# Two single-batch groups at the ends of a 16-batch pipeline, and the last batch's keys and values behind the batch ahead of it

## The chip, the core and the metric

The kernel runs on one core of a Trainium2 chip. The metric is device time in microseconds (us), the median of the runs of the whole program; lower is better. Before the change it is 1442.21 us (three runs, 1441.21 to 1450.63). Engine names are those of the profile: PE is TensorE (matmuls), PEld its weight loads, DVE is VectorE, ACT is ScalarE, POOL is GpSimd, SP is SyncE, which issues nearly all transfers.

## The reference, cut to what matters

Two layers work on 16 batches of 112 tokens with 512 channels, all in float32. Layer 0 is cross-attention from the tokens to 375 context rows of the same batch; layer 1 is one recurrent block (RWKV-like) over the 112 tokens.

```python
# layer 0: 16 heads of 32
a = layer_norm(ctx) * gamma + beta
Q, K, V = x @ Wq.T, a @ Wk.T, a @ Wv.T
x = x + tanh(gate) * (softmax(Q K^T * scale, masked) V) @ Wo.T
# layer 1: 32 heads of 16, state s of 16 x 16 for each head
xa = ln(x, ln1);  sx = shift(xa) - xa            # "front"
xxx = tanh((xa + sx * maa_x) @ maa_w1) @ maa_w2   # five mixes
xk, xw, xv, xr, xg = xa + sx * (maa_stack + xxx)
w = exp(-exp(time_decay + tanh(xw @ td_w1) @ td_w2))
r, k, v, g = xr @ Wr.T, xk @ Wk.T, xv @ Wv.T, silu(xg @ Wg.T)
out_t = r_t . (u * k_t v_t + s);  s = k_t v_t + w_t * s   # "middle", over 112 tokens
x1 = x + (group_norm(out) * g) @ Wo.T             # "back"
xc = ln(x1, ln2);  xk2, xr2 = mixes of xc and its shift
return x1 + sigmoid(xr2 @ Wfr.T) * (relu(xk2 @ Wfk.T)**2 @ Wfv.T)
```

A batch depends on no other batch. Nothing in a layer-1 stage can start before layer 0 has finished for all batches of its group.

## The kernel before, in words

**Tiles.** Tokens lie along the free dimension and channels along the 128 partitions, in four chunks (`NC`). Layer 1 works on groups of `GB` = 2 batches, so on `N` = 224 columns; there are `NG` = 8 groups. A 512 x 512 weight is used in two halves; each call of `project` (L175) loads one half (512 KB, a "slab", five buffers) and runs 8 products, each of which the profile shows as two PE instructions, 16 in all. Ten weights go through `project`: `wq`, `wo` (layer 0), `wk1`, `wv1`, `wr1`, `wg1`, `wo1`, `wfk`, `wfr`, `wfv` (layer 1). A group thus takes 20 calls and 320 instructions.

**Attention** (`attention`, L383) goes batch by batch in four steps of four heads. The context of the batch ahead is turned, and its keys and values are made, in eleven units (`context_units`, L214: four turns, four keys, three values) that are dealt out over the four steps of the current batch; queries of the next group join them (`query_units`, L261). Scores run at L301, transposes of the probabilities at L332, outputs at L351, keys at L237, values at L248. When the last batch of a group has been divided by its sums (`divide`, L358), `project_units` (L274) applies `wo` for the group and adds to `x` at L281; from then on layer 1 of the group may begin.

**Layer 1** has three stages, each a generator for a group: `front` (L517: norm, shift, five mixes), `middle` (L648: four projections, then 16 steps `n`), and `back` (L835: second half of the group norm, `wo1`, second norm, `wfk`, `wfr`, `wfv`, output). A step of `middle` reads a value row back from DRAM spread over 16 partitions (four transfers on SP, L722), multiplies it by the keys (L735, half on DVE and half on POOL), runs the recurrence as scans (L758 on DVE, two scans of two columns with 2 x 224 elements each), multiplies by `r` (L762 on POOL) and sums by matmul (L774). The wide tiles of `front` and `back` have one buffer for each name, so a group's second norm (tile "kk", L848) waits until the group ahead has used its own "kk" in `wfv`.

**Order.** One loop (L919) writes out all work in one sequence. Every generator yields costs; each of the four strands (attention, front, middle, back) has a place on one axis, and the strand with the smallest place goes next. Attention moves 1/92 for each unit of cost (`ATT`), a stage moves its length divided by its listed cost: lengths 0.35, 0.75, 0.8 for front, middle, back (L41). A stage of group g starts no earlier than the place where the stage before it ended, and each strand does one group at a time. For the group ahead of the last, `AHEAD_OF_LAST` (L43) shortens front to 0.25 and middle to 0.6. The framework lays out each engine's static order from this sequence; an instruction whose inputs are ready can be put ahead of earlier ones that are not. `planned_after` adds order without a wait. SP issues weights, contexts and the spreads of L722 in one queue.

Of the kernel before, what the change touches and what calls it, by code (L numbers as in the profile page):

```python
# [18 lines left out]
GB = 2  # L19
NG = B // GB  # L20
# [22 lines left out]
AHEAD_OF_LAST = {"front": 0.25, "middle": 0.6}  # L43
# [6 lines left out]
def xattn_rwkv_kernel(ctx: ExitStack, tc: tile.TileContext, ins: dict, out: bass.AP):  # L50
    nc = tc.nc

    def planned_after(later, earlier):

        tc.add_manual_dep(
            later.ins, earlier.ins.name,
            mybir.DependencyInfo(
                mybir.DependencyClass.NoSync, mybir.DependencyReason.SCHED_ONLY
            ),
            reason="room in the static order",  # L60
        )

# [73 lines left out]
    def load_x(g):  # L136
        xt = xp.tile([P, NC, N], F32, tag="x", name=f"x_{g}")
        nc.sync.dma_start(xt, ins["x"][:, :, g * N : (g + 1) * N])
        return xt

    def load_first():

        xt = xp.tile([P, NC, N], F32, tag="x", name="x_0")
        w = slabs.tile([P, NC, 2 * P], F32, tag="slab", name="wq_0")
        for k in range(NC):
            nc.sync.dma_start(xt[:, k, :], ins["x"][:, k, 0:N])
# [28 lines left out]
    def project(name, mm, rhs, label):  # L175

        w = first.pop(0) if first else slab(name, mm)
        ps = mm_tile(label)
        for e in range(2):
            for k in range(NC):  # L180
                mm_ = nc.tensor.matmul(  # L181
                    ps[:, e * N : (e + 1) * N], w[:, k, e * P : (e + 1) * P], rhs[:, k, :],
# [4 lines left out]
        return ps[:, : 2 * N].rearrange("p (e n) -> p e n", e=2)  # L187
# [73 lines left out]
    def query_units(g):  # L261
        qTs[g] = qT = kvp.tile([P, NC, N], F32, tag="qT", name=f"qT_{g}")
# [26 lines left out]
    def scores(b, m):  # L289
# [6 lines left out]
        qT, kT, mb, t0 = qTs[b // GB], kTs[b][m], masks[b], (b % GB) * T  # L296
# [61 lines left out]
    def divide(b, oR):  # L358
# [16 lines left out]
        t0 = (b % GB) * T  # L375

        with tc.high_priority(AHEAD):
            nc.vector.tensor_tensor(
                qTs[b // GB][:, :, t0 : t0 + T], pb[:, : NC * T].rearrange("p (m t) -> p m t", m=NC), oR,
# [3 lines left out]
    def attention():  # L383
# [3 lines left out]
        for cost, unit in queries[:1] + keys_values[:2] + queries[1:] + keys_values[2:]:  # L387
# [5 lines left out]
        for i in range(NC * B + 2):  # L393
            b, m = divmod(i, NC)
            if i < NC * B:
                if m == 0:
                    g = b // GB
                    if b % GB == 0 and g + 1 < NG:
                        xg[g + 1] = load_x(g + 1)
                    if b + 1 < B:  # L400
                        units += context_units(b + 1)
                        if (b + 1) % GB == 0:
# [6 lines left out]
                yield 0.9  # L409
            copied = None  # L410
# [5 lines left out]
            if i < NC * B:  # L416
# [3 lines left out]
            todo = -(-len(units) // (NC - m)) if i < NC * B else len(units)  # L420
            mine, units = units[:todo], units[todo:]
            mine = mine + [(0.0, lambda: None)] * (3 - len(mine))
            if ready and bm == NC - 1:
# [5 lines left out]
                if bb % GB == GB - 1:  # L429
                    mine = mine[1:2] + project_units(bb // GB) + mine[2:]  # L430
# [15 lines left out]
            before = (b, m, prs) if i < NC * B else None  # L446
# [5 lines left out]
    def wide(tag, name, bufs=1):  # L452
        return big.tile([P, NC, N], F32, tag=tag, name=name, bufs=bufs)

    def duo(tag, name, bufs=2):
        return chk.tile([P, 2, N], F32, tag=tag, name=name, bufs=bufs)

    def small(name):
        return tmp.tile([P, 2, N], F32, tag="tmp", name=name)
# [18 lines left out]
    def over_chunks(t):  # L478
        return t.unsqueeze(1).broadcast_to([P, NC, N])

    def layer_norm(src, dst, sq, late, name):
# [11 lines left out]

        halves(dst, src)
        yield 2.5
        mean = mm_tile(f"{name}_mean")[:, :N]
# [7 lines left out]
        var = mm_tile(f"{name}_var")[:, :N]  # L504
        total(var, sq)
        yield 1
        r = inverse_std(flat(small(f"{name}_r"))[:, :N], var)
        for cc in range(2):
            d2 = dst[:, two(cc), :]
            nc.vector.tensor_tensor(d2, d2, r.unsqueeze(1).broadcast_to([P, 2, N]), ALU.mult)  # L510
# [6 lines left out]
    def front(g):  # L517

        x = xg[g]
        xa, sx = wide("xa", f"xa_{g}"), wide("sx", f"sx_{g}")  # L520
        yield from layer_norm(x, xa, wide("mx", f"sq_{g}"), g == NG - 1, f"ln1_{g}")
        for c in range(NC):
# [9 lines left out]
            by_batch(sx)[:, :, :, 0], st01[:, 1, :, g * GB : (g + 1) * GB],  # L532
# [3 lines left out]
        mix = wide("mx", f"mx_{g}")  # L536
# [7 lines left out]
        for k in range(NC):  # L544
            nc.tensor.matmul(
                ps[:, :N], maa1[:, k, 0 : 4 * DM], mix[:, k, :], start=(k == 0), stop=(k == NC - 1)
# [477 lines left out]
```

## Time and profile before

| what | value |
|---|---|
| median of the runs | 1442.21 us |
| profiled execution, its own time | 1444.43 us |
| its span, first to last instruction | 1442.7 us |
| PE busy | 1344.5 us, 93% |
| DVE busy | 916.1 us, 63% |
| ACT, POOL busy | 658.8 and 660.8 us, 46% each |
| mean granted PE clock | 0.968 |
| moved by DMA | 171.80 MB, mean 119 GB/s |

Stages, read from when the lines ran: the first front follows the first `project_units` of layer 0 (L281 at 135 us); scans of the eight groups begin at 203, 355, 523, 688, 856, 1024, 1186 and 1316 us. In the steady part a group takes 167 us. The last group's L281 is at 1235 us, its scans run 1316 to 1394, and the program ends at 1442.7. Busy time of PE is the sum of modelled durations; the idle rest of the span is 98.2 us.

### The profile page before, as it was taken

Reading aid. Unit: us, or ns where it says so; the run is one execution under the profiler, and the core shown is the slowest. Engines: PE = TensorE matmul, PEld = TensorE weight load, DVE = VectorE, ACT = ScalarE, POOL = GpSimd, SP = SyncE. Lnnn points to the kernel's source line nnn. Section 1 sums busy time; section 2 is a strip of 40 time slices with the busy share of each in tenths; the row PEclk is TensorE's granted clock in tenths of the full one; section 3 lists DMA queues with packets and bytes.
Section 4 is the critical chain, followed back from the end, with each engine's and each line's share of the span. In section 5 each row is a group of like instructions: output and inputs, shape, how many; then the busy total and the mean of one; then the engine's idle time right before and its main releaser. Section 6 shows DMA issues by size and latency. Waiting matters only on the chain.

```text
span 1442.7 us, 23371 instructions
## 1 busy us (share of the span) xinstructions
PE 1344.5 (93%) x8516; PEld 953.6 (66%) x8516; DVE 916.1 (63%) x1750; ACT 658.8 (46%) x1527; POOL 660.8 (46%) x643
## 2 busy tenths in 40 slices
PE   7999998999999999999999999999999898789767
PEld 5557575757686677757676575866777476568546
DVE  1344647883768656774667837785658647884852
ACT  1444532564435653464435634365434446412342
POOL 3001335642546346552556335553456426664750
PEclk9999999999999999999999999999999999889979
DMA  7112035413545045522655035440544033435541
GB/s 233 57 52 82 2 103 153 152 47 97 163 146 162 30 143 170 154 87 73 181 155 158 31 109 173 131 155 30 175 156 156 32 104 126 157 110 150 174 139 57
DMA packets 114666, 171.80 MB, mean 119 GB/s; under 512 B 9768, under 2 KB 87464, under 8 KB 114296
## 3 DMA queue, kind: packets, MB, share of 16 engines
q1 hardware_dynamic: 113912, 169.69, 38.3%
q8 instruction: 67, 1.10, 0.3%
q10 hardware_dynamic: 576, 0.52, 0.1%
q14 instruction: 47, 0.39, 0.1%
q0 software_dynamic: 64, 0.10, 0.0%
HBM read 162.95 MB, written 7.34 MB: 118 GB/s over the span
## 4 chain that ended last, share of the span: by engine, by line
PE 68%; DVE 13%; DMA 5%; ACT 5%; POOL 4%; issue 3%; SPq 2%; DVEq 0%; POOLq 0%; ACTq 0%
PE pk L237 9%; PE pv L248 9%; PE pt L332 5%; PE ps L301 5%; DVE st L758 4%; PE pfv L181 3%; PE pfr L181 3%; PE po L181 3%; PE acc L774 3%; PE pq L181 3%; DMA kv<-vd 3%; PE pfk L181 3%; PE pr L181 2%; PE po L351 2%; PE pv L181 2%
## 5 line engine op out<-in xcount | busy, mean ns | idle before, releaser
L762 POOL TENSOR_TENSOR st<-st,r 128x448 f32<-128x448 f32 x256 | 321.4, 1270 | 213.1 <-DVE st L758 202.8
L758 DVE TENSOR_TENSOR_SCAN st<-wp,kv 128x448 f32<-128x448 f32 x256 | 268.1, 1077 | 112.1 <-ACT qT L268 33.3
L735 POOL TENSOR_TENSOR kv<-kv,k 128x444 f32<-128x444 f32 x128 | 153.4, 1201 | 92.0 <-DMA kv<-vd 90.0
L237 PE MATMUL pk<-aT,wk 128*128 128x375 f32 x512 | 181.6, 499 | 11.7 <-ACT oR L356 10.8
L248 PE MATMUL pv<-wv,aT 128*125 128x512 f32 x384 | 175.0, 599 | 1.4 <-ACT v L253 0.9
L312 DVE CUSTOM_DVE_ANT_0 pr<-ps,mb 112x375 f32<-112x375 f32 x256 | 128.1, 543 | 56.4 <-PE ps L301 56.2
L321 ACT ACTIVATE pr<-pr,mn 112x375 f32<-112x375 f32 x256 | 153.3, 602 | 4.8 <-DVE mn L312 4.6
L237 PEld LDWEIGHTS pk<-aT,wk 128*128 128x128 f32 x512 | 96.5, 196 | 69.6 <-ACT oR L356 12.6
L332 PEld LDWEIGHTS pt<-ident,pr 112*125 112x125 f32 x768 | 104.1, 192 | 36.8 <-issue 16.3
L332 PE MATMUL pt<-ident,pr 112*125 112x112 f32 x768 | 115.1, 281 | 6.1 <-DVE xm L562 5.7
L248 PEld LDWEIGHTS pv<-wv,aT 128*125 128x125 f32 x384 | 68.4, 187 | 77.2 <-issue 73.9
L735 DVE TENSOR_TENSOR kv<-kv,k 128x444 f32<-128x444 f32 x128 | 108.4, 847 | 1.4 <-DMA kv<-vd 1.3
L774 PE MATMUL acc<-st,consts 128*32 128x224 f32 x1024 | 78.0, 373 | 10.9 <-POOL st L762 9.4
L301 PE MATMUL ps<-kT,qT 32*112 32x375 f32 x512 | 84.1, 521 | 1.8 <-DVE xm L562 0.9
L470 ACT ACT_TABLE_LOAD x64 | 82.1, 1283 | 1.1
L568 POOL TENSOR_TENSOR xm<-xm,xa 128x448 f32<-128x448 f32 x48 | 59.0, 1244 | 37.6 <-DVE xm L562 37.5
L341 DVE COPY prT<-pt 125x448 f32<-125x448 f32 x80 | 49.2, 615 | 42.0 <-PE pt L332 41.9
L339 ACT COPY prT<-pt 125x448 f32<-125x448 f32 x112 | 59.1, 528 | 28.2 <-PE pt L332 28.1
L293 POOL TENSOR_SCALAR mb<-mrow 112x375 f32<-112x375 uint8 x16 | 8.9, 558 | 131.4 <-DVE mn L312 128.0
L562 DVE SCALAR_TENSOR_TENSOR xm<-pxm,vecs,sx 128x224 f32<-128x224 f32 x128 | 47.4, 443 | 28.2 <-PE pxm L585 28.1
L243 ACT COPY kT<-pk 128x375 f32<-128x375 f32 x64 | 30.1, 470 | 73.1 <-PE pk L237 72.4
L181 PE MATMUL pfk<-xk,wfk 128*128 128x224 f32 x256 | 53.8, 362 | 9.8 <-DVE xk L861 4.2
(146 smaller groups left out, 2367.2 us busy)
## 6 DMA issues: line engine op xcount, KB each, us to landing
kv<-vd SPq DMA_DIRECT2D x512, 111.5 KB
wo<-in_wo SPq DMA_DIRECT2D x32, 512.0 KB
ctx<-in_ctx SPq DMA_DIRECT2D x15, 750.0 KB
wv<-in_wv SPq DMA_DIRECT2D x16, 512.0 KB
wk<-in_wk SPq DMA_DIRECT2D x16, 512.0 KB
wr<-in_wr SPq DMA_DIRECT2D x16, 512.0 KB
wg<-in_wg SPq DMA_DIRECT2D x16, 512.0 KB
wfk<-in_wfk SPq DMA_DIRECT2D x16, 512.0 KB
```

The lines of the kernel that those rows point to most:

```text
L181: mm_ = nc.tensor.matmul(ps[:, e * N : (e + 1) * N], w[:, k, e * P : (e + 1) * P], rhs[:, k, :], start=(k == 0), stop=(k == NC - 1),)
L237: nc.tensor.matmul(pk[:, :S], wk[:, k, m * P : (m + 1) * P], aT[:, k, :], start=(k == 0), stop=(k == NC - 1),)
L248: nc.tensor.matmul(pv[:SC, :], aT[:, k, c * SC : (c + 1) * SC], wv[:, k, :], start=(k == 0), stop=(k == NC - 1),)
L301: score = nc.tensor.matmul(ps[:T, :S], qT[r : r + HD, m, t0 : t0 + T], kT[r : r + HD, :], start=True, stop=True,)
L312: nc.vector.tensor_tensor_reduce(pr, pss[hh][:T, :S], mb, 1.0, 3.0e38, ALU.add, ALU.min, mn)
L321: exp = nc.scalar.activation(pr, pr, AF.Exp, bias=mns[b][:, h : h + 1], scale=-1.0, accum_out=dens[b][:, h : h + 1],)
L332: nc.tensor.transpose(pt[:SC, hh * T : (hh + 1) * T], prs[hh][:, c * SC : (c + 1) * SC], ident[:T, :T])
L470: nc.scalar.preload_act_table_set(table)
L735: product = engine.tensor_tensor(kv4[:, two(p), :, 1:T], kv4[:, two(p), :, 1:T], k_prev.unsqueeze(1).broadcast_to([P, 2, GB, T - 1]), ALU. ...
L758: scan = nc.vector.tensor_tensor_scan(flat(pair), w_ps[c], flat(kv[:, two(p), :]), 0.0, ALU.mult, ALU.add)
L762: nc.gpsimd.tensor_tensor(pair, pair, rs[c // 2][:, c % 2, :].unsqueeze(1).broadcast_to([P, 2, N]), ALU.mult,)
L774: part = nc.tensor.matmul(accs[c][32 * q : 32 * q + 32, :], consts[:, C_WIN + 32 * e : C_WIN + 32 * e + 32], st[:, q, :], start=(e == 0), ...
```

## The change

Groups now have sizes 1, 2, 2, 2, 2, 2, 2, 2, 1: nine groups, {0}, {1,2}, {3,4}, ..., {13,14}, {15}. Everything that had 224 columns has 112 in the first and last group. A scan still works on 448 elements: for one batch it takes four columns at once (`nw` = 4), so a step of `middle` has one scan and one product with `r` instead of two. The number of spread transfers (four a step) and of slabs (20 a group) stays, so there are 64 more spreads, of half the size, and 20 more slabs than before.

The last batch's context units and its group's queries are no longer dealt out over the steps of batch 14. They are written after batch 14's last step: three in the first of two step-less turns of the loop, ten in the second: one ahead of `divide`, one between it and the two `project_units` calls of group {13,14}, eight behind these. Batch 14's steps carry no such units.

In the planner, the shortened lengths hold for two groups, {11,12} and {13,14}, and are 0.2 and 0.5; lengths of a one-batch group are halved. At the start, both query calls are written ahead of the first turns.

```diff
-GB = 2
-NG = B // GB
+SIZES = (1, 2, 2, 2, 2, 2, 2, 2, 1)
+NG = len(SIZES)
+FIRST = [sum(SIZES[:g]) for g in range(NG)]
+GROUP = [g for g in range(NG) for _ in range(SIZES[g])]
+GB = max(SIZES)
...
-AHEAD_OF_LAST = {"front": 0.25, "middle": 0.6}
+AHEAD_OF_LAST = {"front": 0.2, "middle": 0.5}
+AHEAD_OF = (NG-3, NG-2)
+
+SINGLE = 0.5
...
+        nt = rhs.shape[-1]
         for e in range(2):
             for k in range(NC):
                 mm_ = nc.tensor.matmul(
-                    ps[:, e * N : (e + 1) * N], w[:, k, e * P : (e + 1) * P], rhs[:, k, :],
+                    ps[:, e * nt : (e + 1) * nt], w[:, k, e * P : (e + 1) * P], rhs[:, k, :],
...
-        for cost, unit in queries[:1] + keys_values[:2] + queries[1:] + keys_values[2:]:
+        for cost, unit in queries + keys_values:
...
-        for i in range(NC * B + 2):
-            b, m = divmod(i, NC)
-            if i < NC * B:
-                if m == 0:
-                    g = b // GB
-                    if b % GB == 0 and g + 1 < NG:
+
+        steps = [divmod(i, NC) for i in range(NC * (B - 1))] + [None, None]
+        steps += [(B - 1, m) for m in range(NC)] + [None, None]
+        for i, step in enumerate(steps):
+            b, m = step or (B - 1, NC - 1)
+            if step:
+                if m == 0 and b < B - 1:
+                    g = GROUP[b]
+                    if b == FIRST[g] and g + 1 < NG:
                         xg[g + 1] = load_x(g + 1)
-                    if b + 1 < B:
+                    if b + 1 < B - 1:
                         units += context_units(b + 1)
-                        if (b + 1) % GB == 0:
+                        if b + 1 == FIRST[g] + SIZES[g]:
                             units += query_units(g + 1)
...
+            elif i < len(steps) - 2 and not units:
+                units = context_units(B - 1) + query_units(NG - 1)
...
+            if step is None and steps[i + 1 : i + 2] == [None]:
+                todo = min(3, todo)
...
+        gb, nt = SIZES[g], SIZES[g] * T
+        nw = NQ // gb
...
-            for p in range(2):
-                pair = st[:, two(p), :]
+            for p in range(NQ // nw):
+                columns = slice(p * nw, (p + 1) * nw)
+                pair = st[:, columns, :]
                 scan = nc.vector.tensor_tensor_scan(
-                    flat(pair), w_ps[c], flat(kv[:, two(p), :]), 0.0, ALU.mult, ALU.add
+                    flat(pair), w_ps[c], flat(kv[:, columns, :]), 0.0, ALU.mult, ALU.add
                 )
...
+    def length_of(name, g, length):
+        if g in AHEAD_OF:
+            length = AHEAD_OF_LAST.get(name, length)
+        return length * (1.0 if SIZES[g] == GB else SINGLE)
```

## The prediction

> **What bounds the kernel now.** I began with the page: the busy table, then the slices.
>
> ```profile
> PE 1344.5 (93%) x8516; PEld 953.6 (66%) x8516; DVE 916.1 (63%) x1750; ACT 658.8 (46%) x1527; POOL 660.8 (46%) x643
> ...
> PE   7999998999999999999999999999999898789767
> ...
> PEclk9999999999999999999999999999999999889979
> ```
>
> PE is the bound, and from the second slice to about the 32nd it has no room: work added there is paid in full, stalls of other engines hardly matter. Idle PE lies at the two ends. To size it I asked for busy time by stage, cut at the points where the stages change hands (columns: length, busy time and instructions of PE, PEld, DVE, ACT, POOL, granted clock, DMA share, GB/s).
>
> ```profile
> 0.00:40.00 40.00, 31.63 (x91) 20.07 (x92) 7.67 (x21) 7.79 (x15) 12.37 (x36) 0.91 0.76 234
> 40.00:1110.00 1070.00, 1037.19 (x6768) 725.97 (x6767) 694.02 (x1394) 520.26 (x1244) 480.31 (x461) 0.99 0.38 115
> 1110.00:1235.00 125.00, 112.47 (x769) 78.93 (x769) 83.10 (x156) 57.41 (x135) 58.14 (x56) 0.93 0.30 96
> 1235.00:1294.00 59.00, 50.67 (x316) 38.00 (x315) 50.07 (x73) 21.90 (x40) 40.43 (x34) 0.88 0.41 130
> 1294.00:1394.00 100.00, 77.50 (x420) 61.26 (x420) 69.77 (x87) 35.63 (x70) 65.03 (x55) 0.90 0.57 176
> 1394.00:1442.70 48.70, 35.04 (x156) 29.42 (x156) 11.44 (x25) 15.76 (x24) 4.48 (x5) 0.89 0.16 50
> ```
>
> Idle PE: 8.4 us at the start, 32.8 in the 1070 us after it (3%), 12.5 up to the last out-projection of layer 0 at 1235, then 44.5 of the last 207.7 us, where the clock falls to 0.89 too. That last stage is a chain, front to middle to back of the last pair; its end stands in the chain of work that ended last:
>
> ```profile
> 1393.27 2.22 POOL st L762 x2
> ...
> 1406.31 4.81 PE po L181 x24
> ...
> 1416.82 2.75 issue
> 1419.57 6.29 PE pfk L181 x32
> 1425.86 6.05 PE pfr L181 x32
> 1431.91 6.07 PE pfv L181 x32
> ```
>
> From the last scan to the end it is one pair's back with nothing beside it: 48.6 us, 18.4 of them three weights with all 224 columns.
>
> **The cost of half width.** Each of the 320 projection instructions of a group now occurs in two groups with 112 columns instead of in one with 224. What each takes is read from the timeline, in runs without a gap:
>
> ```profile
> 1317.04 3.19 PE L181 MATMUL po<-o,wo 128*128 128x224 f32 x16
> 658.66 0.95 PEld L332 LDWEIGHTS pt<-ident,pr 112*125 112x125 f32 x8 [0.64 <-DVE xm L562]
> 658.66 1.12 PE L332 MATMUL pt<-ident,pr 112*125 112x112 f32 x8 [0.30 <-DVE xm L562]
> ```
>
> 224 columns: (3.19 - 0.36 of the last one) / 15 = 189 ns. The nearest row with 112 columns and nearly full weights: (1.12 - 0.27) / 7 = 121 ns, its weight loads (0.95 - 0.19) / 7 = 109 ns, which is also the median from start to start over the trace. So the weight load is the floor, and I take 110. Two halves cost 220 instead of 189: 320 x 31 ns = 9.9 us. Bounds: 95 ns (the transposes of L370) give nothing; 140 ns give 29 us. The Trainium skill ("TensorE: Matmul & The Clock Gate", "LDWEIGHTS" and "Back-to-back issue gap") prices a load at its columns / 1.2 GHz and a warm product at N / 2.4 + 2.5 ns. Its load agrees (107 ns for 128 columns), but by its product 224 columns would take 96 ns, so both widths would sit on the load and halving would cost 320 x 107 = 34 us. The row has 189 ns for 224 columns, so the row decides. Other matmuls of a group (`acc`, `pth`, `pw`, norms) come in fours or are few: +1 us, by the same ratio. About half of these 11 us fall into the saturated beginning, undiminished.
>
> **Other added work, counted at nothing.** ACT: some nine table loads (L470, 1.28 us) and four decay exponentials a chunk instead of two, about 13 us for the extra group; ACT is half idle beside PE. If that cover went it would cost those 13 us. DVE, POOL: a scan of four columns has the same 448 elements (1.08 us), a one-batch step has one scan and one product with `r` (1.27 us); no more elements in all. DMA: 20 slabs of 512 KB more, at a mean share of 38%. Spreads: 892 bytes become 444 a packet. The skill ("DMA: Bandwidth & Descriptors", "Specifications") wants 512 bytes for full rate, which speaks against the change. In this trace 375-byte packets took a median 22 ns and 892-byte ones 41, so 444 bytes should take about 25. Even at 41 ns a step's 512 packets are 512 x 41 / 16 engines = 1.3 us, below what SP needs to issue its four transfers:
>
> ```profile
> L722 SPq DMA_DIRECT2D kv<-vd x512: 574/575/3559, 194.4 to 1378.4; - x171
> ```
>
> With the gap between them four issues are 4 x 0.617 = 2.5 us, and 16 steps 39.5 us. That is the floor of a one-batch middle. Behind a spread waiting for its buffer on SP stand the slabs of `wg1` and of back; with five buffers ahead I add nothing.
>
> **The start.** x of the first group is half as long (224 KB less at 234 GB/s, 1 us), but 2.5 us of query work that filled a wait for context and keys go as well. Nothing in sum, -2 to +2.
>
> **The end.** I counted the PE work in the written order, each matmul at its start-to-start time, and set the places of the strands out by the loop's rule. Before, 1073 of 1205 counted us stand ahead of the last out-projection, which came at 1235. After, 1115 of 1215 do: batch 15's keys and values (22 us) moved behind batch 14, and the compressed lengths put {13,14}'s front and half its middle ahead. At the same rate it comes at 1235 + 42 x 1235/1073 = 1283. At this point (place 7.49), 8 of the 16 steps of middle {13,14} remain (it ends at 7.70). Before, a step took 108/16 = 6.8 us beside attention and 78/16 = 4.9 without; at 5.6, they end at 1328. Front {15} (7.66) ends just ahead, as it did before (last pd at 1289 against last scan at 1294).
>
> Behind 1328 there are two chains. First, {15} itself: from last scan to first scan 22 us before, of which about 12 were PE and ACT work that halves: 16. Then 16 steps: DVE needs 1.08 + 0.45 + 0.1 us a step, 26 in all, beside some 20 us of back {13,14}; SP needs 39.5 plus slabs; I take 48. Then its back: 48.6 less 7.7 for `pfk`, `pfr`, `pfv` (18.4 x 79/189) less about 5.5 for `po`, norms and elementwise work: 35. Sum 1328 + 99 = 1427. Second, backs in series, because "kk" has one buffer: back {11,12} ends at place 7.94 of the last middle's 7.70 to 8.06, so 16 + 31 us behind 1328; back {13,14} then needs from its second norm to `pfv` 28 us as before plus 2 for company; back {15} from its second norm 19: 1328 + 96 = 1424. As the two interfere I add 2 to the later: span 1429.
>
> As a ledger: busy 1344.5 + 11 - 3 (fewer half-clock us in a shorter end) = 1352.5. Idle 8.4 + 33 + 12.5 as before, leaving 22.6 of the last 146 us, against 44.5 of 207.7: 85% busy instead of 79%. The profiled execution's own time is 1444.43 for its span of 1442.7, and the median is 1442.21; so the median stands 0.5 below the span: 1428.
>
> **The rivals.**
> - *The end shrinks more* (0.17): front and middle {15} run at their floors (36 + 15 + 43) and the clock stays up. Stage of 130 us instead of 146: 1411. For it: the ledger has 22 us idle left. Against it: DVE was busy 70 of the 100 us after 1294 with 33.5 of scans alone, so a one-batch middle beside a pair's back still fills it to some 90%.
> - *No gain* (0.07): middle {13,14} doesn't keep its shortened places, because DVE is 85% busy already between 1235 and 1294; the extra 11 us and later steps eat the 13 us. 1441.
> - *Backs end in series, slower* (0.12): written order has back {13,14} begin at 7.99, almost where the last middle ends (8.06). If it isn't pulled ahead, 16 + 48 us of the last middle are followed by the rest of back {13,14} (15 + 28) and 19 of back {15}: 1328 + 126 = 1454, with a colder clock 1458. It decides from about 14 us of back {13,14} behind the last scan. Against it: the static order takes ready work ahead of unready work, and back {13,14} needs only middle {13,14}, whose norm the last scans don't touch.
> - *Half width buys nothing* (0.06): 112 columns take 189 ns as 224 do, since loads aren't hidden. 320 x 189 = 60 us instead of 10: half in the beginning, the rest mostly in the end, 1472. Equal to before at 150 ns. Against it: the 109 ns above.
>
> **How the numbers follow.** The likeliest case (0.58) spans 1415 to 1445. A median of three can tell about 1%: 1427.8 and 1456.6. Case one lies on both sides of the lower line, 0.28 below. Faster 0.28 + 0.17 = 0.45; same 0.30 + 0.07 + 0.01 = 0.38; slower 0.11 + 0.06 = 0.17. The range leaves out most of the last rival and the better part of the first: 1406 to 1460.
>
> **What would show it.** Right: projections of the outer groups at about 110 ns from start to start; last L281 near 1283; scans of the last pair ending near 1328, the last group's 16 scans within 43 to 52 us; under 36 us from last scan to end; PE busy near 1352. Wrong: L281 late (then the written-order count failed), a gap over 20 us ahead of the last scans, `pfv` of {13,14} behind the last scan, or PE busy over 1365.

## The result and the profile after

The changed kernel takes 1505.72 us (four runs, 1502.72 to 1512.34); the kernel before, with the runs made beside it, has a median of 1445.79. The ratio is 1.042 (95% interval 1.039 to 1.045): slower by 60 us, where 1428 was predicted and 1460 was the end of the range. The profiled execution, the slowest of the four, has a span of 1510.6 us.

The page of the changed kernel, in the lines that were shown of before:

```profile
PE 1394.4 (92%) x9080; PEld 989.4 (66%) x9080; DVE 932.0 (62%) x1838; ACT 683.9 (45%) x1622; POOL 666.3 (44%) x679
...
PE   8989999998999999999999999999899899868677
...
PEclk9999999899999999999999999999999899888888
```

PE is busy 49.9 us longer and idle 18.0 us longer (116.2 against 98.2). In the slices the tail of low digits is longer and at a lower clock than before. Early on there are eights of PE in the first, third and tenth slice and of the clock in the eighth; before, PE had a seven in the first and an eight in the seventh, and the clock nines up to the 34th.

Where along the stream does the loss come in? A mark that both kernels have is the last `divide` of batch 12 (L378 before, L394 after): by then PE has done the same work, but for the extra group. Busy time on each side of that mark, before and after (columns: length; busy time and instructions of PE, PEld, DVE, ACT, POOL; granted clock; DMA share; GB/s):

```profile
0.00:1013.50 1013.50, 974.88 (x6272) 675.88 (x6273) 635.95 (x1297) 485.06 (x1148) 438.76 (x447) 0.99 0.38 116
1013.50:1442.70 429.20, 369.61 (x2245) 277.77 (x2244) 280.11 (x453) 173.69 (x379) 222.00 (x196) 0.92 0.41 127
```

```profile
0.00:1050.10 1050.10, 1005.08 (x6562) 700.26 (x6563) 644.27 (x1340) 493.12 (x1197) 444.79 (x470) 0.98 0.40 119
1050.10:1510.60 460.50, 389.28 (x2519) 289.15 (x2517) 287.71 (x499) 190.75 (x426) 221.47 (x210) 0.89 0.40 124
```

The stretch to batch 12 is 36.6 us longer, the rest 31.3. The first number is the surprise: the prediction had given the start "nothing in sum". The first 311 us hold it, to the divide of batch 3: 45.4 us later than before. PE has done 377 more instructions by then, but only 290 more at the mark, so some of layer 1 has come sooner, and 9 of the 45 us are got back by batch 12.

The stages of the end, by the same view: from the mark to the last out-projection of layer 0 (L297, the former L281), to 1381 (the front of {15} is done; the decay product of its middle, L718, starts at 1382.6), to the last scan, to the end:

```profile
1050.10:1325.00 274.90, 252.47 (x1637) 177.23 (x1637) 188.37 (x330) 119.87 (x277) 149.12 (x136) 0.94 0.39 123
1325.00:1381.00 56.00, 39.11 (x277) 26.54 (x270) 46.16 (x76) 26.74 (x47) 35.53 (x35) 0.79 0.40 122
1381.00:1438.50 57.50, 42.84 (x313) 34.07 (x311) 36.28 (x54) 20.75 (x59) 32.04 (x34) 0.86 0.52 155
1438.50:1510.60 72.10, 54.86 (x300) 51.31 (x300) 16.90 (x42) 23.40 (x43) 4.78 (x6) 0.83 0.32 103
```

Behind the last scan there are 72 us, with PE busy for 55 of them. The chain of work that ended last tells whose work this is (columns: start, length, what):

```profile
1437.41 1.10 DVE st L789
...
1440.37 7.55 PE po L197 x32
...
1456.62 7.98 PE pfk L197 x32
1464.60 6.05 PE pfr L197 x32
1470.65 6.07 PE pfv L197 x32
1476.77 0.04 issue
1476.81 0.62 DVE rr L917
1477.43 0.31 DVE o L655
...
1482.43 5.26 PE po L197 x24
...
1494.01 5.50 PE pfk L197 x32
1499.51 3.57 PE pfr L197 x32
1503.09 3.59 PE pfv L197 x32
```

The whole back of {13,14}, from its `wo1` at 1440, comes behind the last scan of {15}; only when DVE has taken its last product (L917) does it turn to the second half of the group norm of {15} (L655). The backs run in series. SP, too, had the slab of `wo1` for {13,14} late: behind eight spreads of {15}, in the order as it was written.

```profile
1425.28 7.06 SPq L752 DMA_DIRECT2D kv<-vd  x8
1432.45 0.88 SPq L169 DMA_DIRECT2D wo<-in_wo  x2
```

Of the four signs that the prediction named for being wrong, three stand in this trace: L297 late (1320 to 1325, not 1283), `pfv` of {13,14} behind the last scan, PE busy over 1365. The fourth was a gap over 20 us ahead of the last scans. Ahead of the scans of {15} there are only 11 us; a gap of 21 us does occur, but inside the middle of {13,14}, ahead of its last four scan pairs (1338.6 to 1359.5).

### The profile page after: what moved, and what is told of

Same layout as the page of the kernel before. It is cut to its first block, busy times and chain, and to the rows that moved or that the text cites. A ratio compares the mean times of both kernels' runs of the same rounds, so it can differ in the third digit from the quotient of the medians.

```text
span 1510.6 us, 25008 instructions
## 1 busy us (share of the span) xinstructions
PE 1394.4 (92%) x9080; PEld 989.4 (66%) x9080; DVE 932.0 (62%) x1838; ACT 683.9 (45%) x1622; POOL 666.3 (44%) x679
## 4 chain that ended last, share of the span: by engine, by line
PE 63%; DVE 12%; DMA 7%; POOL 5%; ACT 5%; issue 4%; SPq 2%; DVEq 0%; ACTq 0%; POOLq 0%
PE pv L264 9%; PE pk L253 7%; DMA kv<-vd 5%; PE ps L317 4%; PE pt L348 4%; DVE st L789 4%; PE po L197 3%; PE pfr L197 3%; PE pfv L197 3%; PE pfk L197 3%; PE pq L197 3%; PE acc L805 3%; PE pr L197 3%; POOL st L793 2%; SPq L752 2%
## 5 line engine op out<-in xcount | busy, mean ns | idle before, releaser
L765 POOL TENSOR_TENSOR kv<-kv,k 128x444 f32<-128x444 f32 (+1 forms) x144 | 156.1, 1086 | 118.5 <-DMA kv<-vd 87.9
L253 PE MATMUL pk<-aT,wk 128*128 128x375 f32 x512 | 185.0, 506 | 15.0 <-ACT oR L372 8.7
L264 PE MATMUL pv<-wv,aT 128*125 128x512 f32 x384 | 179.0, 608 | 1.0 <-ACT v L269 0.6
L765 DVE TENSOR_TENSOR kv<-kv,k 128x444 f32<-128x444 f32 (+1 forms) x144 | 121.4, 843 | 6.5 <-DMA kv<-vd 6.5
L317 PE MATMUL ps<-kT,qT 32*112 32x375 f32 x512 | 98.6, 540 | 4.6 <-ACT prT L355 1.9
L805 PE MATMUL acc<-st,consts 128*32 128x224 f32 (+1 forms) x1152 | 83.7, 357 | 13.8 <-POOL st L793 12.3
L493 ACT ACT_TABLE_LOAD x72 | 92.4, 1283 | 1.3
L592 POOL TENSOR_TENSOR xm<-xm,xa 128x448 f32<-128x448 f32 (+1 forms) x54 | 60.2, 1131 | 63.8 <-DVE xm L586 63.8
L586 DVE SCALAR_TENSOR_TENSOR xm<-pxm,vecs,sx 128x224 f32<-128x224 f32 (+1 forms) x144 | 49.5, 416 | 34.9 <-PE pxm L609 34.9
L805 PEld LDWEIGHTS acc<-st,consts 128*32 128x32 f32 x1152 | 26.0, 111 | 63.8 <-issue 31.3
L197 PE MATMUL pfk<-xk,wfk 128*128 128x224 f32 (+1 forms) x288 | 59.7, 365 | 8.5 <-issue 6.0
```

What stands on the lines that cost most here:

```text
L197: mm_ = nc.tensor.matmul(ps[:, e * nt : (e + 1) * nt], w[:, k, e * P : (e + 1) * P], rhs[:, k, :], start=(k == 0), stop=(k == NC - 1),)
L253: nc.tensor.matmul(pk[:, :S], wk[:, k, m * P : (m + 1) * P], aT[:, k, :], start=(k == 0), stop=(k == NC - 1),)
L264: nc.tensor.matmul(pv[:SC, :], aT[:, k, c * SC : (c + 1) * SC], wv[:, k, :], start=(k == 0), stop=(k == NC - 1),)
L317: score = nc.tensor.matmul(ps[:T, :S], qT[r : r + HD, m, t0 : t0 + T], kT[r : r + HD, :], start=True, stop=True,)
L493: nc.scalar.preload_act_table_set(table)
L765: product = engine.tensor_tensor(kv4[:, two(p), :, 1:T], kv4[:, two(p), :, 1:T], k_prev.unsqueeze(1).broadcast_to([P, 2, gb, T - 1]), ALU. ...
```

## The experiments

Eighteen kernels ran, each timed in three rounds beside the kernel before on the same chip. Times are medians. Ratios are to the kernel before; "the mark" is the divide of batch 12 (1013.5 before, 1050.1 after).

The expectations name theories by letter. A is the first theory: half width along the stream, and the backs in series at the end. B puts the loss on the moved keys and values, C on the four-column step of the last middle. D says that the price belongs to a one-batch group as such. P, the packing theory, was formed after the first runs: a one-batch group has half the columns but as many serial steps as a pair, and `SINGLE = 0.5` writes them into half the places, so that PE meets steps that aren't ready.

### First: the parts of the change one by one

**The keys and values alone.** Eight pairs as before; only the last batch's context units are written behind batch 14. (The code is that of the changed kernel with `SIZES` of twos; lengths, queries and the order of the start are as before. Only the first lines of the edit are shown.)

```diff
-SIZES = (1, 2, 2, 2, 2, 2, 2, 2, 1)
+SIZES = (2, 2, 2, 2, 2, 2, 2, 2)
...
```

> Eight groups of two and the old lengths, as before; only the last batch's keys and values are moved behind the end of batch 14's steps. Theory A: within 8 us of the kernel before (1437 to 1453), since the work is the same and lies where TensorE is full. Rival B: 1465 us or more. Rival C: no change.

Measured: 1445.26, ratio 1.001 (0.999 to 1.002). By itself this part changes nothing, so B is out, and neither does the changed code as such.

**One-batch groups at the start alone.** Two of them, so that the tail is that of the kernel before; order of the start, lengths of the group ahead of the last and keys and values as before.

```diff
-SIZES = (1, 2, 2, 2, 2, 2, 2, 2, 1)
+SIZES = (1, 1, 2, 2, 2, 2, 2, 2, 2)
-AHEAD_OF_LAST = {"front": 0.2, "middle": 0.5}
-AHEAD_OF = (NG-3, NG-2)
+AHEAD_OF_LAST = {"front": 0.25, "middle": 0.6}
+AHEAD_OF = (NG-2,)
...
```

> Groups of one, one, and seven times two: both small groups at the start, none at the end; the last batch's keys and values dealt out over batch 14 and the planner's lengths as in the kernel before. Theory A (the loss has two sites: some 27 us at the start, from half-width projections, a colder clock and rwkv work in the saturated stretch, and some 35 us at the end, where the last two backs run one after the other): 1465 to 1475 us, and batch 12 divided 25 to 40 us later than before. Rival B (the moved keys and values do it, since the scans stand still while TensorE makes them) and rival C (the four-column scan does it): at most the 11 us of half-width loads, 1457 or less.

Measured: 1508.86, ratio 1.042 (1.038 to 1.047). Two small groups at the start cost as much as the whole change. The mark stands at 1087.2, and the rest is as long as before (427.4 against 429.2 us, with 2246 PE instructions against 2245):

```profile
0.00:1087.20 1087.20, 1028.10 (x6836) 716.32 (x6837) 645.93 (x1385) 515.68 (x1246) 440.84 (x483) 0.97 0.38 118
1087.20:1514.60 427.40, 368.14 (x2246) 276.55 (x2244) 278.72 (x454) 173.99 (x379) 220.84 (x196) 0.93 0.40 128
```

So the loss is no matter of the end alone: 74 us for two one-batch groups at the start, 37 for one, as in the changed kernel. Theory A had 1465 to 1475 and falls here; B and C had 1457 or less.

**Two columns a step in the last middle**, as before the change:

```diff
-        nw = NQ // gb
+        nw = 2
```

> The changed kernel, with two columns in a scan for one batch too (two scans of 224 elements in a step instead of one of 448). Rival C (one scan a step needs both halves of the product, so scan, product with r and next product follow one another, 3.1 us a step): the 16 scans of {15} shrink from 49 to 35 to 40 us and the time falls by 9 to 15 us to 1490 to 1496. Theory A: within 6 us of 1505, since the back of {13,14} behind it sets the end anyway.

Measured: 1505.43, ratio 1.042 (1.038 to 1.045). The 16 steps take 49.7 us with two columns and 49.6 with four. The four-column step is neither a gain nor a loss here; C is out.

**The last backs sooner.** The changed kernel, with a shorter length for the last four backs, so that the back of {13,14} is written ahead of the last middle's end:

```diff
     def length_of(name, g, length):
         if g in AHEAD_OF:
             length = AHEAD_OF_LAST.get(name, length)
+        if name == "back" and g in (NG-4, NG-3, NG-2, NG-1):
+            length = 0.45
```

> The changed kernel, with the planner's length of back shortened from 0.8 to 0.45 for the last four groups, so that back of {13,14} is written beside the scans of {15} and not behind them. Theory A: last scan to end falls from 72 us to 35 to 50, the time from 1505 to 1475 to 1490. Rivals B and C: what back gains there is lost elsewhere, within 6 us of 1505.

Measured: 1517.49, ratio 1.049 (1.046 to 1.053), 11 us worse than the changed kernel. Theory A had 1475 to 1490, and the rivals had no more than 6 us of change. The edit did what it was meant to: `wo1` of {13,14} runs at 1411 to 1421, beside the beginning of the last middle, and from the last scan to the end it is 46 us instead of 72. But the last divide slips from 1317 to 1340 and the last scan from 1438 to 1468. The series of backs is what the trace shows last, and taking it away is paid for ahead of it.

**Half width by itself.** A kernel of eight pairs whose projections of groups 2 to 5 run in two halves of 112 columns. No more groups, slabs or steps; 320 more PE instructions for each of four groups.

```diff
         for e in range(2):
-            for k in range(NC):
-                mm_ = nc.tensor.matmul(
-                    ps[:, e * nt : (e + 1) * nt], w[:, k, e * P : (e + 1) * P], rhs[:, k, :],
...
+            for j in range(parts_):
+                for k in range(NC):
+                    mm_ = nc.tensor.matmul(
+                        ps[:, e * nt + j * wide_ : e * nt + (j + 1) * wide_],
+                        w[:, k, e * P : (e + 1) * P], rhs[:, k, j * wide_ : (j + 1) * wide_],
...
```

> The kernel before, where every projection of groups 2 to 5 is done in two halves of 112 columns (as many half-width instructions as two one-batch groups have, for each of four groups), and nothing else. It measures the disputed price by itself. My count of 31 ns for a pair of halves: 320 x 31 ns x 4 = 40 us, 1480 to 1490. If half-width projections alone explain the 33 us or so that a one-batch group costs (twice that for a pair's worth): 4 x 50 or more, above 1600. If their price is hidden: 1450 or less.

Measured: 1473.82, ratio 1.020 (1.016 to 1.024): 29 us over before (1445.04 there), 7.2 us a group, 23 ns for each pair of halves. The prediction had 31 ns and 9.9 us, and 1480 to 1490 was expected here. What it called the price of half width is real, and too small to carry 60 us.

### Second: the places

**Full places for the one-batch groups.** The changed kernel with one number changed: a one-batch group gets the places of a pair. Its instructions are the same.

```diff
-SINGLE = 0.5
+SINGLE = 1.0
```

> The changed kernel, with a one-batch group given as many places in the written order as a pair (SINGLE 1.0 instead of 0.5), so that its chains lie more thinly among the attention. Theory P (packing: the half-length places put a one-batch group's chain of small steps so close that TensorE meets it unready, with waits, scattered scores and a half-rate clock): 1475 to 1490 us instead of 1505, half-rate clock time down by 20 us or more. Theory D (the price belongs to a one-batch group as such: half-width projections, smaller bursts, one more pass of every fixed step): 1500 to 1512.

Measured: 1473.77, ratio 1.020 (1.016 to 1.023): 32 us, over half of the loss, come back, and D is out for that half. Busy time on each side of the mark:

```profile
0.00:1024.90 1024.90, 986.34 (x6562) 691.46 (x6563) 639.94 (x1340) 496.08 (x1199) 445.75 (x470) 0.99 0.40 122
1024.90:1472.40 447.50, 386.29 (x2519) 285.44 (x2517) 285.80 (x499) 190.45 (x426) 220.22 (x210) 0.91 0.41 127
```

Up to the mark, the same 6562 PE instructions as in the changed kernel take 1024.9 us instead of 1050.1. 18.7 us of the difference are PE's busy time, 6.5 are idle. The scores have 11.3 of the 18.7 (80.6 us of busy time against 69.2). Their rows in the stretch up to batch 3, first of the changed kernel, then of this one (columns: line, engine, operation, tiles, shape, count; busy us, mean ns of one; idle before):

```profile
L317 PE MATMUL ps<-kT,qT 32*112 32x375 f32 x136 | 32.3, 566 | 0.5 <-DVE prT L357 0.2 <-DVE xm L586 0.2
```

```profile
L317 PE MATMUL ps<-kT,qT 32*112 32x375 f32 x136 | 21.6, 549 | 0.0
```

One score takes as long in both; but 136 of them cover 10.7 us more, since fewer of them run at the same time.

The 25 us are not all the order's. Of the runs below, "full at the end" has the changed kernel's order up to the mark, and its mark is at 1045.0; "full at the start" has it at 1022.8. First full places at the end only, then at the start only:

```profile
0.00:1045.00 1045.00, 997.67 (x6562) 698.27 (x6563) 644.37 (x1340) 492.91 (x1197) 445.38 (x470) 0.99 0.40 120
```

```profile
0.00:1022.80 1022.80, 983.80 (x6562) 690.40 (x6563) 641.93 (x1340) 496.14 (x1199) 446.39 (x470) 0.99 0.40 123
```

So the first group's places are worth 22 us up to the mark, 13.9 of them busy, of which the scores have 7.8. The other 5 of the changed kernel's profiled execution go with its clock: the granted clock in these traces is either 1.0 or 0.5, and up to the mark PE was busy at 0.5 for 46 us there, against 30 with full places at the end. At the end, too, `pfk` to `pfv` of {13,14} now run at 1413 to 1439, beside the last middle, and 38 us instead of 72 follow the last scan, while the 16 steps take 64 us instead of 50.

**The start alone with 0.9.** The kernel with two one-batch groups at the start, with one number changed:

```diff
-SINGLE = 0.5
+SINGLE = 0.9
```

> Groups of one, one, and seven times two, all else as before the change (as in the run with both small groups at the start, 1509 us), with SINGLE 0.9 instead of 0.5. Theory P: 1475 to 1490. Theory D: 1500 to 1512.

Measured: 1490.30, ratio 1.031 (1.027 to 1.036), 0.3 us over what P expected. The mark comes at 1057.6 instead of 1087.2: 22 us for each one-batch group, where 0.5 cost 37.

**The keys and values dealt out as before.** The changed kernel, with batch 15's context units and queries over the steps of batch 14:

```diff
-        steps = [divmod(i, NC) for i in range(NC * (B - 1))] + [None, None]
-        steps += [(B - 1, m) for m in range(NC)] + [None, None]
+        steps = [divmod(i, NC) for i in range(NC * B)] + [None, None]
...
-                    if b + 1 < B - 1:
+                    if b + 1 < B:
```

> The changed kernel, with the last batch's keys and values dealt out over the steps of batch 14 as before. If moving them does no good in this setting either: within 8 us of 1505. If it is what keeps the end from being worse: 1515 or more. If the scans' pause from 1226 to 1277 us comes from it: 1490 or less.

Measured: 1514.95, ratio 1.050 (1.045 to 1.055), so in this kernel the move may be worth some 9 us, although alone it was worth nothing. The intervals of the two ratios only just touch, so this is not firm.

**Start and end apart.** Full places for the first one-batch group only, and for the last only:

```diff
-        return length * (1.0 if SIZES[g] == GB else SINGLE)
+        return length * (1.0 if SIZES[g] == GB or g == 0 else SINGLE)
```

> The changed kernel with full places for the first single group's front, middle and back; the last single group keeps half places. With full places for both the time was 1474, 32 us below the changed kernel's 1506, and batch 12's divide (the mark of the start) came at 1025 instead of 1050. Packing theory: the first group's share is what that mark shows, so batch 12 again near 1025 here, and 1480 to 1487. Rival, that the gain is all in the last group's places and the start only follows by chance: batch 12 near 1050 and over 1498.

```diff
+        return length * (1.0 if SIZES[g] == GB or g == NG - 1 else SINGLE)
```

> The counterpart: full places for the last single group alone, half places for the first. Packing theory: batch 12's divide stays near 1050; from it to the end some 449 instead of 460 us, the last back overlapping the last middle (under 45 us behind the last scan instead of 72): 1493 to 1502. Together with the other half the gains should come to 32 us, within 6. Rival, that the gain is the last group's alone: 1470 to 1480.

Measured: 1484.94, ratio 1.026 (1.021 to 1.030), with the mark at 1022.8; and 1498.74, ratio 1.036 (1.030 to 1.042), with the mark at 1045.0. The gains are 21 and 7 us and come to 28 of the 32 for both; the 7 are within the noise, as the interval overlaps that of the changed kernel (1.039 to 1.045). The larger part of the cost of the places is at the start.

**The last middle alone.** Full places for the first group and the middle of the last, half places for the last front and back:

```diff
+        return length * (1.0 if SIZES[g] == GB or g == 0 or name == "middle" else SINGLE)
```

> Full places for the first group and for the middle of the last; half places for the last group's front and back. If it is the middle of the last group that must not be packed, it ends as with full places or better, since front 15 comes sooner: 1466 to 1476. If its front or its back is what costs, no better than full places for the first group alone: 1480 to 1490.

Measured: 1480.04, ratio 1.023 (1.018 to 1.028): at the very edge of the second case, 1480 to 1490, and with an interval that overlaps those of full places for the first group alone and for both. So it doesn't say which of the last group's stages minds its places.

**Full places and two columns a step:**

```diff
-SINGLE = 0.5
+SINGLE = 1.0
...
-        nw = NQ // gb
+        nw = 2
```

> Full places for both single groups, and the last middle's loop over two columns at a time (as before the change) instead of four. At half places the two loops took the same time, where the end was given by backs in series. Here the last middle lies nearer the end: 16 steps of 4.1 us. If four columns with their product split over two engines hold those steps up, two columns give 1462 to 1470; if the steps are held up by the supply and by TensorE's other work, the same 1474 within 5; if the fewer, wider instructions are a gain, 1478 to 1485.

Measured: 1467.88, ratio 1.015 (1.010 to 1.020). The interval overlaps that of full places with four columns, and the spans of the two profiled executions are 1471.9 and 1472.4: no difference is shown.

### Third: places taken from a pair

Is it the places, or do they cost only together with half width? The kernel before has no half width. One group of it was packed:

```diff
-                todo[name] = (part(g), (AHEAD_OF_LAST.get(name, length) if g == NG - 2 else length) / us)
+                packed = 0.5 if g == 3 else 1.0
+                todo[name] = (part(g), packed * (AHEAD_OF_LAST.get(name, length) if g == NG - 2 else length) / us)
```

> The kernel before with one edit: front, middle and back of group 3 (batches 6 and 7) are written out in half their places. No instruction is added, nothing has half width. Packing theory: TensorE meets steps that aren't ready and, behind them, attention with nothing beside it: 10 to 35 us slower, 1456 to 1481, with the loss between the divides of batches 8 and 12 and more half-rate clock there. Rival, that packing hurts only through half-width instructions: within 5 of 1446.

Measured: 1484.39, ratio 1.023 (1.019 to 1.027): some 34 us over before (1450.7 there) and 3 over the range, without one instruction more. From the divide of batch 7 to that of batch 12, first the kernel before, then this one:

```profile
598.40:1013.50 415.10, 403.53 (x2643) 284.37 (x2642) 279.90 (x542) 212.17 (x483) 202.21 (x191) 0.99 0.39 120
```

```profile
598.80:1054.60 455.80, 421.57 (x2643) 294.78 (x2643) 278.73 (x543) 209.94 (x481) 200.38 (x191) 0.96 0.35 109
```

The same 2643 PE instructions take 40.7 us longer: 18.0 busy and 22.7 idle, at a clock of 0.96 instead of 0.99. The waits of PE in this stretch are many and small, none over 5 us in sum, on DVE, POOL and ACT by turns. The scores have only 2.1 of the 18.0 us (29.1 against 27.0). More of it goes with the clock: up to the mark PE was busy at 0.5 for 47 us here, against 25 before, which is about 11 us of longer busy time if the half clock doubles it (an estimate). The divide of batch 8 is already 40 us late (718.6 against 678.3), earlier than expected, with 120 more instructions done by then; from there to batch 12 it takes as long as before (336.0 against 335.2 us) with 121 fewer.

The same edit for the first pair (`g == 0`):

> The same for group 0 (batches 0 and 1) of the kernel before. Packing theory: the half-packed single group cost 25 us at the mark of batch 12 (1050 against 1025); a pair has twice the work in its places, so at least that: 1466 to 1490, batch 12's divide 1035 to 1055 instead of 1013. Rival: within 5 of 1446, batch 12 near 1013.

Measured: 1485.45, ratio 1.024 (1.023 to 1.026), the mark at 1054.8. And for the last (`g == NG - 1`):

> The same for the last group (batches 14 and 15) of the kernel before. Behind the last out-projection nothing but this group and the pair ahead of it is left, so its places only set what goes first. Packing theory, as for the last single group (7 us for full places): 1446 to 1458, with the loss behind 1235. Rival, that sooner places for the last group bring the end forward: 1435 to 1443.

Measured: 1461.38, ratio 1.008 (1.004 to 1.012), so 11 us, 3 over what P expected. The start pays more than the end, as in the changed kernel, where half places cost 21 us at the start and 7 at the end.

### Fourth: more places

If too few places were all, more would help on. The changed kernel with two columns a step and 1.15 times a pair's places for the first group (1.0 for the last):

```diff
+        return length * (1.0 if SIZES[g] == GB or g == NG - 1 else 1.15)
```

> The changed kernel with 1.15 times a pair's places for the first single group, a pair's places for the last, and two columns a step in the last middle. The like with 1.0 for both gave 1468 (ratio 1.0147), batch 12's divide at 1025 against 1013 before. If a single group still has too few places: batch 12 at 1017 to 1021 and 1458 to 1464 (ratio 1.007 to 1.012). If what is left there is half width and more instructions: the same, 1463 to 1473, batch 12 near 1025.

Measured: 1489.77, ratio 1.032 (1.027 to 1.037), against 1.015 with 1.0 for both, and beyond both cases that were expected. The mark comes at 1047 instead of 1024.9, with the same 6562 instructions: almost all that full places had given back is lost again. The counterpart, 1.15 for the last group:

```diff
+        return length * (1.0 if SIZES[g] == GB or g == 0 else 1.15)
```

> The counterpart: 1.15 for the last single group, 1.0 for the first, two columns a step. Theory that its places are still too few: the last middle's steps stay where they are (DVE and the supply set them), the back comes later: 1460 to 1467. Theory that at the end places only delay what would be ready: 1470 to 1478.

Measured: 1468.49, ratio 1.017 (1.014 to 1.020): as with 1.0, between the two cases. And the kernel before, with 1.15 for all groups:

```diff
-                todo[name] = (part(g), (AHEAD_OF_LAST.get(name, length) if g == NG - 2 else length) / us)
+                todo[name] = (part(g), 1.15 * (AHEAD_OF_LAST.get(name, length) if g == NG - 2 else length) / us)
```

> The kernel before with 1.15 times the places for front, middle and back of every group. PE is 97% busy in the middle of the stream, so more places can give back at most the 3% idle there, 30 us, of which most is the rhythm of attention itself; and the last group ends later by what its strands are stretched. Packing theory: the old lengths lie near the flat bottom: 1440 to 1455. If the pairs too were packed too closely: 1425 to 1438. If stretching pushes the end out: 1456 to 1475.

Measured: 1538.93, ratio 1.065 (1.061 to 1.069), 64 us beyond the worst that was expected. In the steady part a pair now takes 184 us instead of 167. PE's waits, the largest over the whole span of this kernel:

```profile
PE pt L332 <- DVE xm L562: 24.1, 8, 4.4
PE pa L222 <- DVE own L701: 21.9, 6, 3.8
PE po L351 <- ACT qT L268: 14.2, 5, 2.9
PE po L181 <- POOL o L645: 11.4, 2, 8.9
```

Before, the wait `pt` had on `xm` was 5.7 us in 13 short pieces, and that of `pa` on `own` was not among the largest. The second number is how often each occurs, and the first two come eight and six times, about once a pair: attention stands behind elementwise work of front and middle at points where it hardly did before. That these waits are what sets the 184 us is read from their count, and was not tried.

This takes "too few places" back to something wider. What is shown is that the order in which the stages are written among each other is worth 20 to 35 us for one group away from the end, with the same instructions, and less for the last group (7 to 11 us with 0.5, none with 1.15). It goes in both directions: for the first one-batch group 0.5 and 1.15 both lose against 1.0; so do 0.5 for one pair and 1.15 for all. P's reason, PE waiting for steps that aren't ready, covers only part of it: most of the difference in the changed kernel, and 18 of 41 us in the packed pair, is busy time of PE.

## Why the prediction was wrong, by its steps

| step | predicted | measured |
|---|---|---|
| start, up to the mark | -2 to +2, and half of 11 for half width | +36.6 (+31.5 in the second trace of this order) |
| last out-projection of layer 0 | 1283 | 1325 |
| then the rest of middle {13,14} | 8 steps, 45 us | 7 steps, 53 us |
| to the first scan of {15} | 16 us | 11 us |
| its 16 scans | 48 us | 49.6 us |
| from the last scan to the end | 35 us | 72 us |
| span | 1429 | 1510.6 |

**The start: the failed step.** "Nothing in sum, -2 to +2" costed the shorter x and the queries, and put the first group's halved lengths at nothing without a reason. The same omission is in "at the same rate it comes at 1235 + 42 x 1235/1073": the count of PE work in the written order was taken as if the rate at which PE gets through it did not depend on how the order mixes the stages. With full places for the first group only, the time falls by 21 us and the mark from 1050 to 1023; what is left of the mark's delay there, 9 us, is busy time of PE (983.8 us against 974.9), with 290 instructions more for the extra group. The 42 us by which L297 was late are those 36.6 and 5 more.

**The ledger's term for the clock: the wrong sign.** It took 3 us off PE's busy time for "fewer half-clock us". There were more: the granted clock was 0.5 for 93 us before and for 147 after, and PE was busy in 80 and 119 of these. A product does take nearly twice as long there, as two score instructions that need 0.88 us at 1.0 show (clock 0.50 from 288 to 296):

```profile
294.22 1.59 PE L317 MATMUL ps<-kT,qT 32*112 32x375 f32 x2
```

Half of the 39 us is 20 us, an estimate of the clock's part of the 49.9 us that PE is busy longer. What makes the clock fall was not tried; part of it is chance, as the two traces of one order show (46 and 30 us of busy time at 0.5 up to the mark).

**The end: a rival's mechanism.** "Its back: 35" assumed that back {13,14} would go beside the last middle, as "the static order takes ready work ahead of unready work". It didn't: the trace has it wholly behind the last scan. The rival of backs in series named this and its point of decision, and gave it 30 us over the likeliest case; at 0.12 it was ranked too low, and alone it would still have given 1458. The experiments also show why the end is a poor place to argue from: writing backs sooner cut the 72 us to 46 and lost 11 in all, and full places for the last group brought 7 only.

**Half width: right, somewhat too dear.** "About 110 ns from start to start" was right:

```profile
1499.35 3.74 PE L197 MATMUL pfr<-xr,wfr 128*128 128x112 f32 x32
```

(3.74 - 0.27 of the last) / 31 = 112 ns. The price of a group, 9.9 us by the sum, measured 7.2 when nothing else changed, within the bounds 0.3 to 29. The row decided rightly over the product time of the Trainium skill ("TensorE: Matmul & The Clock Gate", "Back-to-back issue gap"): the 34 us a group estimated from it would have made the four split groups 136 us slower, not 29.

**Other engines, transfers, the one-batch middle: right as far as shown.** The 16 scans came within the 43 to 52 us. SP's floor of 39.5 lay below the 49.6 that they took. The half-sized packets took a median 25 ns, as estimated, and the pace of a step was 3.1 us, which two columns a step did not change. That the 13 us of ACT work had their cover along the stream is likely, and no run of its own shows it. In the one place where they had less, between 1337 and 1360, ACT loads its table seven times (9.0 us) while the middle of {13,14} pauses; that these loads make the pause was not tried.

**What stays open.** With the best places found, the change is still slower by 21 to 29 us (ratios 1.015 to 1.020). Between full places and before, PE has 564 instructions and 28 us of busy time more, and the idle time is nearly the same (99.8 against 98.2). Half width explains some 7 of these 28, and the half clock some 5 (an estimate: PE busy at 0.5 for 91 us against 80). The rest wasn't separated; other products with fewer columns and products of layer 1 that are cut up further among attention's may be in it. Nor was a mixture of lengths for all groups looked for, and no version here beats the kernel before.

## What to carry to other kernels

Where a written order weaves several serial chains around a saturated engine, the lengths that space them are part of the kernel's tuning, and an edit that resizes one chain has to be costed as a change of that order, along the whole stream and not only at the end it aims at. Compare stretches with the same instruction count between two marks: if they differ in length, it is not the work, but the order or the clock. Two traces of one order differed by 5 us here, so a smaller difference says nothing. And don't halve a chain's room because its work halves: the number of its steps stays, and here half the room cost more than it saved.

## What was not expected of the hardware

**"Busy" is no measure of work when products share the array.** A step of attention has four heads, so four scores, each with 32 rows of weights of its own (`32*112` in the rows below) and each shown as two PE instructions. In the kernel before, all eight instructions together took 0.90 us; in the changed kernel the two of one head, alone between other products, took 0.88, and those of two heads 0.89:

```profile
121.49 0.90 PE L301 MATMUL ps<-kT,qT 32*112 32x375 f32 x8
```

```profile
151.12 0.89 PE L317 MATMUL ps<-kT,qT 32*112 32x375 f32 x4
...
152.52 0.88 PE L317 MATMUL ps<-kT,qT 32*112 32x375 f32 x2
```

One instruction takes some 0.5 us, so eight in 0.90 us ran four or more at a time; when the order parts the heads, one takes as long as four. That the two instructions of a head follow each other while the heads overlap is read from these times. All 512 score instructions cover 84.1 us before and 98.6 after (a part of it by the clock), at nearly the same mean of one (521 and 540 ns). So reordering can add busy time, and a profile with PE at 95% in a stretch can still have lost there.

**The clock can fall in a stretch in which PE is hardly idle, and less in another trace of the same order.** From 40 to 311 us of the changed kernel the mean granted clock is 0.94 with PE busy 256.71 of 271.1 us; with full places at the end, in the same order up to there, it is 0.97 from 40 to 305.1 us with 249.59 of 265.1; in the kernel before, from 40 to 265.7, it is 0.98 with 215.82 of 225.7. The busy shares are 95, 94 and 96%. By the Trainium skill ("TensorE: Matmul & The Clock Gate", "The HAM clock gate") the gate looks at how busy the array has been of late; what the profile calls busy didn't tell these stretches apart.
